# Row-order dt kept in SBUF, permutes in other slots, and the residual summed in PSUM, in a two-layer Metaformer kernel

## The chip, the cores and the metric

The kernel runs on one core of a Trainium2 chip. Five engines work side by side, each through its own queue of instructions in order: TensorE (PE, matmuls), VectorE (DVE), ScalarE (ACT), GpSimd (POOL) and SyncE (SP), which here issues nearly all DMAs. They wait for each other by semaphores. The metric is the device time of a whole execution in microseconds (us), the median over several runs.

## The reference

The input is one image of 64×64 positions with 96 channels. Layer 0 and layer 1 each add a mixer with state-space scans and then an MLP. The change lies in layer 1, whose mixer is, cut to what matters:

```python
xz = x @ W_in.T                                   # 96 -> 2 x 192
xp, z = xz[..., :192], xz[..., 192:]
xc = silu(conv3x3(xp) + conv_b)                   # dense, 192 -> 192 channels
xs = [row order, column order, and both reversed] # 4 sequences of L = 4096
dts, Bs, Cs = split(x_proj_w @ xs, [6, 16, 16])
delta = softplus(dt_proj_w @ dts + dt_proj_b)     # "dt", one per channel and position
A = -exp(A_logs)                                  # 192 x 16 states
# for each sequence, step by step:
h = exp(delta * A) * h + delta * u * B            # 16 states per channel
y = sum(h * C over states) + D * u
# the four sequences' y are put back in row order and added
out = (yy * silu(z)) @ W_out.T                    # 192 -> 96, "out_proj"
x = x + out                                       # the residual
```

The MLP after it normalizes x, rounds to eight-bit and sixteen-bit floats and adds its result to x.

## The kernel before, in words

**Stages.** Layer 0 comes first. Layer 1 then computes the convolution and, in `project_chunks`, the projections, softplus, dt and du (= u·dt), in two halves of 32 image rows: chunks of 512 positions (`CH`), four to a half. `project_chunks` goes through `for i in range(3)`: i = 0 and 1 are channels 0 to 127 in the first and second 1024 positions of the half, i = 2 is channels 128 to 191 of all 2048, folded on the partitions. It writes dt (row order, and `dtc` in column order), du, B and C to DRAM. The scan stage `scans` reads them again, and the `tail` does out_proj of the last channels and the MLP.

**Scan stage.** The 192 channels are cut in 6 groups of 32 (`NG`, `GC`), the 16 states in quarters: a tile has 32 channels × 4 states on its 128 partitions, and a group takes 4 passes, 24 passes in all (numbered 0 to 23). One pass has 16 slots, and one slot is one DVE scan of 128×1024 values (`tensor_tensor_scan`, L1261):

| slots | what is scanned | written to |
|---|---|---|
| 0–3 | columns, one way | h1s |
| 4–7 | columns, the other way | xws, in place |
| 8–11 | rows, one way | h0s |
| 12–15 | rows, the other way | x0s, x1s or x2s, in place |

`xs[i % 3]` holds B·du of pass i in row order (x0s, x1s, x2s in the trace); xws is its copy in column order, made by `permute` (L1240) in four parts. Each scan needs a decay factor `da` = exp(A·dt), made by ACT from dt1s (column order) or dt0s (row order) in PSUM with two buffers (`decay`, L1250); slots 4 and 12 use the one of the slot before.

**Around the scans.** In each pass, POOL adds the two column scans to hss, back in row order (`add_columns`, L1266, four parts, from h1s and xws). PE adds hss, h0s and x through an identity matrix into PSUM (`add_all`, L1274, tile `hs`, two buffers), ACT copies that out (`fetch`, L1280), POOL multiplies by C (`times_c`), and PE sums the states (`sum_states`). POOL also multiplies B by du for coming passes (`times_b`, L1234).

**Order.** The order on each engine is written out by hand: `keep` holds an instruction in program order on its engine. A table `plan` says in which slot, counted from a pass's own slot 0, each step is issued; a negative slot lies in the pass before, one of 16 or more in the pass after. In each slot the scan is issued first, then `decay` of the next slot, then what the plan lists:

```python
spots(permute, -7, -6, -5, -4)        # ACT, for the next pass: its slots 9 to 12
spots(add_columns, 5, 6, 7, 8)        # POOL
spots(add_all, 13, 15, 18, 20)        # PE, fetches of ACT between slots 15 and 24
```

**Pass 0.** Before the first scan, dt1s of group 0 is spread from `dtc` within SBUF to the four partitions of each channel (`spread`, L1058 to L1060), and dus from du likewise. dt0s of group 0 is loaded from DRAM, by `load_dt(0, 0)` (L1439), four DMAs of 512 KB issued by SP after all stores. SP's DMAs are taken in order: those of `project_chunks`, then these.

**Early out_proj.** In passes 17 to 23, y of the finished groups is read back (`load_y`, tile ye), multiplied by its weights (`early_out`, L1381, tile eo), copied by ACT (`early_fetch`, L1386, tile et) and added by POOL to the residual `res` (`early_add`, L1389). f = 0 stands for channels 0 to 127 from pass 17 on, two chunks to a pass, f = 1 for the next 32 from pass 21 on, three to a pass. Channels 160 to 191 follow in the tail.

Of the kernel before, what the change touches and what calls it, by code (L numbers as in the profile page):

```python
# [108 lines left out]
class Net:  # L109
# [24 lines left out]
    def column(self, name, value):  # L134
        t = self.cp.tile([P, 1], F32, tag=name, name=name)
        self.nc.gpsimd.memset(t, value)
        return t
# [550 lines left out]
    def softplus(self, sp, z, dt, n, name, last=None):  # L688

        nc = self.nc  # L690
        nc.scalar.activation(z, z, AF.Sigmoid, bias=self.nln2, scale=-1.0)
        zz = sp.tile([P, n], F32, tag="zz", name=f"zz{name}")
        nc.scalar.activation(zz, z, AF.Square)
        p = sp.tile([P, n], F32, tag="p", name=f"p{name}")
        nc.vector.tensor_scalar(p, zz, LOG1P[4], None, ALU.mult)
        for i in (3, 2, 1):
            nc.vector.scalar_tensor_tensor(p, p, LOG1P[i], zz, ALU.add, ALU.mult)
        nc.vector.scalar_tensor_tensor(p, p, LOG1P[0], z, ALU.add, ALU.mult)
        (last or nc.vector).tensor_tensor(dt, dt, p, ALU.add)

        return p
# [220 lines left out]
    def layer1(self, w, pool):  # L922
        nc, tc = self.nc, self.tc
        self.bc_d = [self.scratch("bc1", [2, NST, L])]
        self.dt_d = [self.scratch(f"dt1{o}", [DI, L]) for o in range(2)]
        self.du_d, self.y_d = self.scratch("du1", [DI, L]), self.scratch("y1", [DI, L])
        self.u_d = [self.scratch(f"u1{g}", [GP[g], L]) for g in range(2)]

        gp = pool.enter_context(tc.tile_pool(name="first", bufs=1))
        self.du, self.dt1 = (gp.tile([P, L], F32, tag=t, name=f"{t}s") for t in ("du", "dt1"))  # L930
        with ExitStack() as ctx:
            dp = ctx.enter_context(tc.tile_pool(name="dtc1", bufs=1))
            sp = ctx.enter_context(tc.tile_pool(name="sp1", bufs=2))
            kp = ctx.enter_context(tc.tile_pool(name="sg1", bufs=3))
            up = [ctx.enter_context(tc.tile_pool(name=f"u1{i}", bufs=1)) for i in range(2)]
# [5 lines left out]
            self.project_chunks(sp, ps, self.conv_chunks(kp, ps, pc, up, 0), 0)  # L941
# [5 lines left out]
            self.project_chunks(sp, ps, u, 4, xs)  # L947
        return xs
# [83 lines left out]
    def project_chunks(self, sp, ps, u, c, xs=None):  # L1032
# [37 lines left out]


        for i in range(3):
# [40 lines left out]
            if xs and i < 2:  # L1113

                for m in range(2):
                    t = ps.tile([P, CH], F32, tag="cw", name=f"du4{i}{m}")
                    nc.tensor.matmul(t, self.spread4, du[0:GC, chunk(m)], start=True, stop=True)
                    x = xs[0][:, chunk(c + first + m)]
                    keep(nc.vector.tensor_tensor(x, x, t, ALU.mult))
            for h in range(1 + g):  # L1120
                r = LANES[h] if g else slice(0, P)
                to = slice(g * P, g * P + r.stop - r.start)
                k = c + first + 2 * h
                at = slice(k * CH, k * CH + n)
                if g == 0:
                    spread(self.du[:, at], du)
                if xs and i == 1:
                    for j in range(1, NS):
                        spread(self.dt1[:, j * SC : (j + 1) * SC], self.dtc[0][:, j * SC : (j + 1) * SC])
                    self.load_b(1, xs[1], half[1])  # L1130
                else:
                    by_column(g, dt[r], k, 1)
                keep(dma(self.dt_d[0][to, at], dt[r]))
                rows = slice(0, GP[1]) if g else slice(GC, P)
                keep(dma(self.du_d[g * P + rows.start : g * P + rows.stop, at], du[r if g else rows]))
        if xs:
            keep(dma(self.dt_d[1][GC:P], self.dtc[0][GC:P]))
            keep(dma(self.dt_d[1][P:DI], self.dtc[1]))
# [21 lines left out]
    def scans(self, xs, out):  # L1160
# [14 lines left out]
        with ExitStack() as ctx:  # L1175
# [7 lines left out]
            st = [inner.enter_context(tc.tile_pool(name=t, bufs=1)) for t in ("dt0", "h1", "xw")]  # L1183
# [8 lines left out]
            dt0, h1, xw = (p.tile([P, L], F32, tag=t, name=f"{t}s") for p, t in zip(st, ("dt0", "h1", "xw")))  # L1192
            du, dt1 = self.du, self.dt1
# [172 lines left out]
            early, inputs, partial, taken = {}, {}, {}, {}  # L1366

            def load_y(f, m):
                rows = (slice(0, P), slice(P, P + GC))[f]
                if f == 0 or m == 0:  # L1370
                    self.ye = gp.tile([P, CH], F32, tag="ye", name=f"ye{f}{m}")
                to = slice(GC * (m % 3), GC * (m % 3) + GC) if f else slice(0, P)
                inputs[f, m] = self.ye[to], self.tail_w[f][to]
                keep(nc.sync.dma_start(self.ye[to], self.y_d[rows, chunk(m)]))

            def early_out(f, m):
                y, w = inputs.pop((f, m))
                t = ph.tile([P, CH], F32, tag="hs", name=f"eo{f}{m}")
                o = t[:, 0 : 4 * CD].rearrange("p (j d) -> p j d", j=4)
                for j in range(4):  # L1380
                    keep(nc.tensor.matmul(o[:, j], y[:, j:CH:4], w, start=True, stop=True))  # L1381
                partial[f, m] = o

            def early_fetch(f, m):
                taken[f, m] = gp.tile([P, 4, CD], F32, tag="et", name=f"et{f}{m}")
                keep(nc.scalar.copy(taken[f, m], partial.pop((f, m))))  # L1386

            def early_add(f, m):
                keep(nc.gpsimd.tensor_tensor(self.res[:, m], self.res[:, m], taken.pop((f, m)), ALU.add))  # L1389
# [36 lines left out]
            spots(permute, -7, -6, -5, -4)  # L1426
# [12 lines left out]
            load_dt(0, 0)  # L1439
# [364 lines left out]
```

## Time and profile before

| | |
|---|---|
| median of 3 runs | 1580.23 us (1579.53 to 1580.86) |
| profiled execution | 1580.6 us |
| its span in the profile | 1578.7 us, 1.9 us lie around it |
| mean granted TensorE clock | 0.81 |
| DVE busy | 1188.7 us (75%) |
| PE busy | 1194.0 us (76%) |
| ACT busy | 890.5 us (56%) |
| POOL busy | 825.9 us (52%) |
| column scans into h1s, 72 of 96 | 169.2 us, 2350 ns each |
| hss adds on POOL | 96 of 2373 ns |

The profile is one execution. Its rows give the start and the time in us, the engine, the line, the tiles written and read (`out<-in`), their shape and, in square brackets, how long the engine was idle before the row and what it was released by. "x4" means four such instructions in one row. SPq rows are DMA issues. The busy shares are means over all stages, so what a change in one stage is worth is read in that stage.

### The profile page before, as it was taken

The numbers are of one execution on the slowest core, as the hardware profiler recorded it, in microseconds if no ns is written. First come the engines' busy times: TensorE is split into PE (matmuls) and PEld (weight loads), VectorE is DVE, ScalarE is ACT, GpSimd is POOL, SyncE is SP. The second block draws the span as 40 slices with busy tenths as digits, with TensorE's granted clock in tenths as the row PEclk, the third lists the DMA queues.
The fourth block names the chain that finished last, engine by engine and source line by source line (L and its number), as shares of the span: only waits on it lengthen the run. The fifth ranks groups of instructions, "written<-read, shape, count | busy, mean of one in ns | idle before, by whom it ended". The sixth has DMA issues, their size and how long they took to land.

```text
span 1578.7 us, 12397 instructions
## 1 busy us (share of the span) xinstructions
PE 1194.0 (76%) x3728; PEld 487.3 (31%) x3728; DVE 1188.7 (75%) x895; ACT 890.5 (56%) x1058; POOL 825.9 (52%) x482
## 2 busy tenths in 40 slices
PE   5969788779999317777777777777777776778875
PEld 2512254434342002222222222222222332333343
DVE  5487344430321859999999999999999998989965
ACT  4233333330422637777777777677777776777535
POOL 1001122110011457776877787777877876886545
PEclk9988666679999558888888888888888887978865
DMA  2032200000132583545555455635564556352201
GB/s 68 1 97 75 56 1 10 21 13 27 23 112 86 150 263 121 183 161 173 150 170 192 141 150 170 202 131 150 170 223 124 158 183 232 120 155 82 83 1 40
DMA packets 65616, 184.20 MB, mean 117 GB/s; under 512 B 21072, under 2 KB 35044, under 8 KB 58596
## 3 DMA queue, kind: packets, MB, share of 16 engines
q1 hardware_dynamic: 63352, 183.03, 37.5%
q8 instruction: 31, 0.51, 0.1%
q10 hardware_dynamic: 2188, 0.29, 0.1%
q14 instruction: 45, 0.37, 0.1%
HBM read 158.07 MB, written 20.99 MB: 113 GB/s over the span
## 4 chain that ended last, share of the span: by engine, by line
DVE 38%; PE 25%; issue 7%; ACT 7%; POOL 5%; DMA 3%; SPq 3%; DVEq 1%; POOLq 0%; ACTq 0%
DVE h1s L1261 10%; DVE xws L1261 10%; DVE h0s L1261 8%; PE hs L1274 5%; PE cv L996 4%; DVE x0s L1261 3%; DVE x2s L1261 3%; DVE x1s L1261 2%; ACT da L1250 2%; ACT xws L1240 2%; PE cv L1001 2%; PE o L455 1%; PE o L454 1%; SPq L1211 1%; PE in L285 1%
## 5 line engine op out<-in xcount | busy, mean ns | idle before, releaser
L1266 POOL TENSOR_TENSOR hss<-h1s,xws 128x1024 f32<-128x1024 f32 x96 | 224.4, 2373 | 139.9 <-PE hs L1274 137.2
L1250 ACT ACTIVATE da<-dt1s,a 128x1024 f32<-128x1024 f32 x168 | 187.8, 1118 | 143.6 <-DVE xws L1261 81.6
L1274 PE MATMUL hs<-hss,ident 128*128 128x512 f32 x376 | 213.1, 650 | 55.8 <-DMA dt0s<-dt 36.0
L1250 ACT ACTIVATE da<-dt0s,a 128x1024 f32<-128x1024 f32 x168 | 187.1, 1115 | 81.2 <-DVE xws L1261 49.6
L1261 DVE TENSOR_TENSOR_SCAN xws<-da,xws 128x1024 f32<-128x1024 f32 x96 | 224.2, 2335 | 8.3
L1274 PE MATMUL hs<-h0s,ident 128*128 128x512 f32 x376 | 198.7, 611 | 14.7 <-DVE h0s L1261 14.7
L1261 DVE TENSOR_TENSOR_SCAN h1s<-da,h1s,xws 128x1024 f32<-128x1024 f32 x72 | 169.2, 2350 | 12.7 <-ACT da L1250 4.5
L1274 PEld LDWEIGHTS hs<-hss,ident 128*128 128x128 f32 x376 | 68.7, 200 | 188.6 <-issue 80.1
L1274 PEld LDWEIGHTS hs<-h0s,ident 128*128 128x128 f32 x376 | 75.0, 200 | 112.9 <-issue 93.8
L1295 PE MATMUL acc<-hc2s,fold 128*32 128x512 f32 x128 | 47.2, 826 | 56.1 <-POOL hc2s L1284 53.0
L1295 PE MATMUL acc<-hc0s,fold 128*32 128x512 f32 x128 | 47.6, 834 | 51.4 <-POOL hc0s L1284 51.4
L1234 POOL TENSOR_TENSOR x2s<-x2s,dus 128x1024 f32<-128x1024 f32 x32 | 75.2, 2360 | 10.9 <-DMA x2s<-bc 10.9
L1295 PE MATMUL acc<-hc1s,fold 128*32 128x512 f32 x128 | 46.1, 810 | 45.8 <-POOL hc1s L1284 45.8
L1261 DVE TENSOR_TENSOR_SCAN x1s<-da,x1s 128x1024 f32<-128x1024 f32 x32 | 74.7, 2335 | 7.5 <-ACT da L1250 5.2
L1261 DVE TENSOR_TENSOR_SCAN x0s<-da,x0s 128x1024 f32<-128x1024 f32 x32 | 74.7, 2335 | 7.2 <-ACT da L1250 4.9
L1112 POOL TENSOR_TENSOR p<-u,dt 128x1024 f32<-128x1024 f32 x6 | 15.1, 2523 | 122.5 <-ACT z L1099 102.7
L1261 DVE TENSOR_TENSOR_SCAN x2s<-da,x2s 128x1024 f32<-128x1024 f32 x32 | 74.7, 2335 | 4.2 <-ACT da L1250 1.7
L1234 POOL TENSOR_TENSOR x1s<-x1s,dus 128x1024 f32<-128x1024 f32 x32 | 75.1, 2359 | 2.6 <-DMA x1s<-bc 2.5
L1274 PE MATMUL hs<-x0s,ident 128*128 128x512 f32 x128 | 67.1, 606 | 0.2 <-DVE x0s L1261 0.2
L1381 PE MATMUL eo<-two,ye 128*128 128x96 f32 (+1 forms) x128 | 30.9, 424 | 48.0 <-DMA ye<-y 37.8
L390 POOL TENSOR_TENSOR ua<-acc,sga 128x512 f32<-128x512 f32 x4 | 5.8, 1453 | 117.2 <-DMA u<-uc 115.5
L1234 POOL TENSOR_TENSOR x0s<-x0s,dus 128x1024 f32<-128x1024 f32 x28 | 65.8, 2363 | 0.0
(310 smaller groups left out, 2628.3 us busy)
## 6 DMA issues: line engine op xcount, KB each, us to landing
c0s<-bc SPq DMA_DIRECT2D x184, 128.0 KB
c1s<-bc SPq DMA_DIRECT2D x184, 128.0 KB
x2s<-bc SPq DMA_DIRECT2D x32, 512.0 KB
x0s<-bc SPq DMA_DIRECT2D x28, 512.0 KB
x1s<-bc SPq DMA_DIRECT2D x28, 512.0 KB
dus<-du SPq DMA_DIRECT2D x20, 512.0 KB
dt1s<-dt SPq DMA_DIRECT2D x40, 256.0 KB
dt0s<-dt SPq DMA_DIRECT2D x40, 256.0 KB
```

Of the source, the lines that this page charges most:

```text
L285: keep(nc.tensor.matmul(t, self.w_in[:, g * P : (g + 1) * P], xt, start=True, stop=True))
L454: keep(nc.tensor.matmul(t[:, j, :], y[0][:, at[0]], w[0], start=True, stop=False))
L996: nc.tensor.matmul(t, cw[0][:, tap, 0:P], image(0, slice(0, P), n, tap), start=tap == 0, stop=False)
L1001: nc.tensor.matmul(t, cw[1][r, tap, 0:P], image(1, r, n, tap), start=False, stop=tap == 8)
L1234: keep(nc.gpsimd.tensor_tensor(x, x, du[:, part[j]], ALU.mult))
L1240: keep(copy(grid(xw)[:, w, :], cols(xs[i % 3])[:, w, :]))
L1250: keep(nc.scalar.activation(das[i, s], dts[o][:, part[j]], AF.Exp, scale=self.a6[:, g, k : k + 1]))
L1261: keep(nc.vector.tensor_tensor_scan(to, da, x, start, ALU.mult, ALU.add))
L1266: keep(nc.gpsimd.tensor_tensor(cols(hs)[:, w, :], grid(h1)[:, w, :], grid(xw)[:, w, :], ALU.add))
L1274: keep(nc.tensor.matmul(t, self.ident, x[:, chunk(m)], start=x is hs, stop=x is xs[i % 3]))
L1295: keep(nc.tensor.matmul(to, self.fold4, src, start=k == 0, stop=k == NK - 1))
L1381: keep(nc.tensor.matmul(o[:, j], y[:, j:CH:4], w, start=True, stop=True))
```

## The change

Five things are changed.

- In `project_chunks`, dt of the first group in row order is spread within SBUF to dt0s, four DMAs for each 1024 positions, as dus is; the load from DRAM before the scans goes, and dt0s moves to the pool "first". Only channels 32 to 127 of dt are stored for the row order. Softplus's instructions are kept in program order (on DVE always, on ACT for i = 0), the last add of dt is done by DVE for i = 2 as well, x_proj of the second two chunks is issued after the first softplus, products of x0s come one round later, and a6 is negated by ACT. The stores of dt and du of i = 1 in the second half come last. du has its own tile.
- In the plan, `permute` is issued three slots earlier for its first part and one slot earlier for the others: in slots 6, 9, 10 and 11 of the pass before.
- In the early out_proj, PE adds the residual by an identity matmul into the same PSUM tile, and ACT copies the sum to `res`; `early_add` and et are gone. ye has two buffers and is loaded in earlier slots.
- The tail's pool has three buffers instead of four.
- The constant columns share a tile.

```diff
@@ -685,20 +687,23 @@
                     nc.sync.dma_start(self.du_d[g][:, at], du)
-    def softplus(self, sp, z, dt, n, name, last=None):
-        nc = self.nc
-        nc.scalar.activation(z, z, AF.Sigmoid, bias=self.nln2, scale=-1.0)
+    def softplus(self, sp, z, dt, n, name, p=None, keep=(None, None)):
+        nc = self.nc
+        act, dve = (k or (lambda instruction: None) for k in keep)
+        act(nc.scalar.activation(z, z, AF.Sigmoid, bias=self.nln2, scale=-1.0))
         zz = sp.tile([P, n], F32, tag="zz", name=f"zz{name}")
-        nc.scalar.activation(zz, z, AF.Square)
-        p = sp.tile([P, n], F32, tag="p", name=f"p{name}")
-        nc.vector.tensor_scalar(p, zz, LOG1P[4], None, ALU.mult)
+        act(nc.scalar.activation(zz, z, AF.Square))
+        if p is None:
+            p = sp.tile([P, n], F32, tag="p", name=f"p{name}")
+        dve(nc.vector.tensor_scalar(p, zz, LOG1P[4], None, ALU.mult))
         for i in (3, 2, 1):
-            nc.vector.scalar_tensor_tensor(p, p, LOG1P[i], zz, ALU.add, ALU.mult)
-        nc.vector.scalar_tensor_tensor(p, p, LOG1P[0], z, ALU.add, ALU.mult)
-        (last or nc.vector).tensor_tensor(dt, dt, p, ALU.add)
-        return p
+            dve(nc.vector.scalar_tensor_tensor(p, p, LOG1P[i], zz, ALU.add, ALU.mult))
+        dve(nc.vector.scalar_tensor_tensor(p, p, LOG1P[0], z, ALU.add, ALU.mult))
+        dve(nc.vector.tensor_tensor(dt, dt, p, ALU.add))
     def scan_group(self, g):
@@ layer1
-        self.du, self.dt1 = (gp.tile([P, L], F32, tag=t, name=f"{t}s") for t in ("du", "dt1"))
+        self.du, self.dt0, self.dt1 = (gp.tile([P, L], F32, tag=t, name=f"{t}s") for t in ("du", "dt0", "dt1"))
...
+            so = ctx.enter_context(tc.tile_pool(name="so1", bufs=2))
@@ -1029,7 +1037,7 @@
         return u
-    def project_chunks(self, sp, ps, u, c, xs=None):
+    def project_chunks(self, so, sp, ps, u, c, xs=None):
@@ -1043,13 +1051,21 @@
                 self.load_b(k, xs[k], half[0])
-        def x_proj(k):
-            h, s = place(k)
-            r = LANES[h]
-            t = ps.tile([P, CH], F32, tag="ps", name=f"xd1{c}{k}")
-            nc.tensor.matmul(t[0:XW], self.w_x[0], u[0][:, chunk(k)], start=True, stop=False)
-            nc.tensor.matmul(t[0:XW], self.w_x[1][r], u[1][r, chunk(s)], start=False, stop=True)
-            nc.scalar.copy(self.xd[:, chunk(k)], t[0:XW])
+        def x_proj(first):
+            for k in (first, first + 1):
+                h, s = place(k)
+                r = LANES[h]
+                t = ps.tile([P, CH], F32, tag="ps", name=f"xd1{c}{k}")
+                nc.tensor.matmul(t[0:XW], self.w_x[0], u[0][:, chunk(k)], start=True, stop=False)
+                nc.tensor.matmul(t[0:XW], self.w_x[1][r], u[1][r, chunk(s)], start=False, stop=True)
+                keep(nc.scalar.copy(self.xd[:, chunk(k)], t[0:XW]))
+            at = slice(first * CH, first * CH + n)
+            here = slice((c + first) * CH, (c + first) * CH + n)
+            for k in range(2):
+                keep(dma(self.bc_d[0][k, :, here], self.xd[(XB, XC)[k] : (XB, XC)[k] + NST, at]))
+            if xs:
+                self.load_b(0, xs[0], here)
         def times_b(j):
...
@@ -1068,22 +1084,20 @@
                 keep(copy(to[:, w], dt[:, w]))
+        late, ready = [], []
+        def product(x, t):
+            return lambda: keep(nc.vector.tensor_tensor(x, x, t, ALU.mult))
         for i in range(3):
...
             bias = self.vec[g][:, 1:2]
-            if i < 2:
-                at = slice(first * CH, first * CH + n)
-                here = slice((c + first) * CH, (c + first) * CH + n)
-                x_proj(first)
-                x_proj(first + 1)
-                for k in range(2):
-                    keep(dma(self.bc_d[0][k, :, here], self.xd[(XB, XC)[k] : (XB, XC)[k] + NST, at]))
-                if xs:
-                    self.load_b(0, xs[0], here)
+            if i == 0:
+                x_proj(0)
             z = sp.tile([P, n], F32, tag="z", name=f"z1{c}{i}")
-            dt = sp.tile([P, n], F32, tag="dt", name=f"dt1{c}{i}")
+            dt = so.tile([P, n], F32, tag="dt", name=f"dt1{c}{i}")
             for m in range(2):
...
@@ -1098,14 +1112,20 @@
                 nc.scalar.activation(dt[:, s], t, AF.Relu, bias=bias)
-            du = self.softplus(sp, z, dt, n, f"1{c}{i}", nc.gpsimd if i == 2 else nc.vector)
+            du = so.tile([P, n], F32, tag="du", bufs=3, name=f"du1{c}{i}")
+            self.softplus(sp, z, dt, n, f"1{c}{i}", du, (keep if i == 0 else None, keep))
+            for f in ready:
+                f()
+            ready = []
+            if i == 0:
+                x_proj(2)
             if xs and i == 0:
...
                 times_b(1)
-            elif xs and i == 2:
+            if xs and i == 2:
                 keep(nc.scalar.activation(self.a6, self.a6, AF.Exp))
-                keep(nc.gpsimd.tensor_scalar(self.a6, self.a6, -1.0, None, ALU.mult))
+                keep(nc.scalar.activation(self.a6, self.a6, AF.Copy, scale=-1.0))
             if xs and i == 1:
...
@@ -1115,25 +1135,32 @@
                     nc.tensor.matmul(t, self.spread4, du[0:GC, chunk(m)], start=True, stop=True)
-                    x = xs[0][:, chunk(c + first + m)]
-                    keep(nc.vector.tensor_tensor(x, x, t, ALU.mult))
+                    ready.append(product(xs[0][:, chunk(c + first + m)], t))
             for h in range(1 + g):
                 r = LANES[h] if g else slice(0, P)
-                to = slice(g * P, g * P + r.stop - r.start)
                 k = c + first + 2 * h
                 at = slice(k * CH, k * CH + n)
-                if g == 0:
-                    spread(self.du[:, at], du)
                 if xs and i == 1:
...
                         spread(self.dt1[:, j * SC : (j + 1) * SC], self.dtc[0][:, j * SC : (j + 1) * SC])
+                    spread(self.du[:, at], du)
                     self.load_b(1, xs[1], half[1])
+                    spread(self.dt0[:, at], dt)
                 else:
+                    if g == 0:
+                        spread(self.du[:, at], du)
+                        spread(self.dt0[:, at], dt)
                     by_column(g, dt[r], k, 1)
-                keep(dma(self.dt_d[0][to, at], dt[r]))
                 rows = slice(0, GP[1]) if g else slice(GC, P)
-                keep(dma(self.du_d[g * P + rows.start : g * P + rows.stop, at], du[r if g else rows]))
+                for d, t in ((self.dt_d[0], dt), (self.du_d, du)):
+                    store = (d[g * P + rows.start : g * P + rows.stop, at], t[r if g else rows])
+                    if xs and i == 1:
+                        late.append(store)
+                    else:
+                        keep(dma(*store))
         if xs:
+            for store in late:
+                keep(dma(*store))
             keep(dma(self.dt_d[1][GC:P], self.dtc[0][GC:P]))
...
@@ -1363,12 +1390,12 @@
                         keep(nc.sync.dma_start(to[q], gu[GC * q : GC * q + GC]))
-            early, inputs, partial, taken = {}, {}, {}, {}
+            early, inputs, partial = {}, {}, {}
             def load_y(f, m):
...
                 if f == 0 or m == 0:
-                    self.ye = gp.tile([P, CH], F32, tag="ye", name=f"ye{f}{m}")
+                    self.ye = gp.tile([P, CH], F32, tag="ye", bufs=2, name=f"ye{f}{m}")
                 to = slice(GC * (m % 3), GC * (m % 3) + GC) if f else slice(0, P)
...
@@ -1377,24 +1404,22 @@
                 o = t[:, 0 : 4 * CD].rearrange("p (j d) -> p j d", j=4)
+                keep(nc.tensor.matmul(o, self.ident, self.res[:, m], start=True, stop=False))
                 for j in range(4):
-                    keep(nc.tensor.matmul(o[:, j], y[:, j:CH:4], w, start=True, stop=True))
+                    keep(nc.tensor.matmul(o[:, j], y[:, j:CH:4], w, start=False, stop=j == 3))
                 partial[f, m] = o
             def early_fetch(f, m):
-                taken[f, m] = gp.tile([P, 4, CD], F32, tag="et", name=f"et{f}{m}")
-                keep(nc.scalar.copy(taken[f, m], partial.pop((f, m))))
-            def early_add(f, m):
-                keep(nc.gpsimd.tensor_tensor(self.res[:, m], self.res[:, m], taken.pop((f, m)), ALU.add))
+                keep(nc.scalar.copy(self.res[:, m], partial.pop((f, m))))
             for f, i0, spots in (
-                (0, n - 7, ((4, 8, 10, 12), (8, 11, 13, 14))),
-                (1, n - 3, ((4, 8, 10, 12), (5, 9, 12, 13), (8, 11, 13, 14))),
+                (0, n - 7, ((0, 8, 10), (2, 11, 13))),
+                (1, n - 3, ((1, 8, 9), (2, 9, 11), (4, 11, 13))),
             ):
...
                     i, s = divmod(m, len(spots))
-                    for do, at_slot in zip((load_y, early_out, early_fetch, early_add), spots[s]):
+                    for do, at_slot in zip((load_y, early_out, early_fetch), spots[s]):
                         early.setdefault((i0 + i, at_slot), []).append((do, (f, m)))
...
@@ -1423,7 +1448,7 @@
             spots(times_b, -20, -19, -16, -14)
-            spots(permute, -7, -6, -5, -4)
+            spots(permute, -10, -7, -6, -5)
             spots(add_columns, 5, 6, 7, 8)
...
@@ -1436,7 +1461,6 @@
             spots(load_c, 10, 12, 18, 21)
-            load_dt(0, 0)
             for j in range(2):
...
@@ -1504,7 +1528,7 @@
-        tp = ctx.enter_context(tc.tile_pool(name="at1", bufs=4))
+        tp = ctx.enter_context(tc.tile_pool(name="at1", bufs=3))
```

More of the change, by code (lines that the diff above doesn't have):

```diff
@@ L134, in column @@
     def column(self, name, value):
-        t = self.cp.tile([P, 1], F32, tag=name, name=name)
+        if not hasattr(self, "columns"):
+            self.columns = iter(self.cp.tile([P, 8], F32, tag="columns", name="columns").rearrange("p (n o) -> n p o", o=1))
+        t = next(self.columns)
         self.nc.gpsimd.memset(t, value)
@@ L929, in layer1 @@
         gp = pool.enter_context(tc.tile_pool(name="first", bufs=1))
-        self.du, self.dt1 = (gp.tile([P, L], F32, tag=t, name=f"{t}s") for t in ("du", "dt1"))
+        self.du, self.dt0, self.dt1 = (gp.tile([P, L], F32, tag=t, name=f"{t}s") for t in ("du", "dt0", "dt1"))
         with ExitStack() as ctx:
             dp = ctx.enter_context(tc.tile_pool(name="dtc1", bufs=1))
+            up = [ctx.enter_context(tc.tile_pool(name="u10", bufs=1))]
+            so = ctx.enter_context(tc.tile_pool(name="so1", bufs=2))
             sp = ctx.enter_context(tc.tile_pool(name="sp1", bufs=2))
             kp = ctx.enter_context(tc.tile_pool(name="sg1", bufs=3))
-            up = [ctx.enter_context(tc.tile_pool(name=f"u1{i}", bufs=1)) for i in range(2)]
+            up.append(ctx.enter_context(tc.tile_pool(name="u11", bufs=1)))
             ps = ctx.enter_context(tc.tile_pool(name="ps_b1", bufs=2, space=PSUM))
@@ L940, in layer1 @@
             self.weights1(up[1], w)
-            self.project_chunks(sp, ps, self.conv_chunks(kp, ps, pc, up, 0), 0)
+            self.project_chunks(so, sp, ps, self.conv_chunks(kp, ps, pc, up, 0), 0)
             u = self.conv_chunks(kp, ps, pc, up, 4)
@@ L946, in layer1 @@
             xs = [xp.tile([P, L], F32, tag=f"x{m}", name=f"x{m}s") for m in range(3)]
-            self.project_chunks(sp, ps, u, 4, xs)
+            self.project_chunks(so, sp, ps, u, 4, xs)
         return xs
@@ L1181, in scans @@
             inner = ctx.enter_context(ExitStack())
-            st = [inner.enter_context(tc.tile_pool(name=t, bufs=1)) for t in ("dt0", "h1", "xw")]
+            st = [inner.enter_context(tc.tile_pool(name=t, bufs=1)) for t in ("h1", "xw")]
             pa = inner.enter_context(tc.tile_pool(name="ps_da", bufs=2, space=PSUM))
@@ L1191, in scans @@
             hs, h0 = (hh.tile([P, L], F32, tag=t, name=f"{t}s") for t in ("hs", "h0"))
-            dt0, h1, xw = (p.tile([P, L], F32, tag=t, name=f"{t}s") for p, t in zip(st, ("dt0", "h1", "xw")))
-            du, dt1 = self.du, self.dt1
+            h1, xw = (p.tile([P, L], F32, tag=t, name=f"{t}s") for p, t in zip(st, ("h1", "xw")))
+            du, dt0, dt1 = self.du, self.dt0, self.dt1
             dts = [dt0, dt1]
```

## The prediction

> **What bounds the kernel now.** I read the page first, then the timelines of one early pass, of the middle of pass 0 and of the late passes, then the waits. On the page:
>
> ```profile
> PE 1194.0 (76%) x3728; PEld 487.3 (31%) x3728; DVE 1188.7 (75%) x895; ACT 890.5 (56%) x1058; POOL 825.9 (52%) x482
> DVE 38%; PE 25%; issue 7%; ACT 7%; POOL 5%; DMA 3%; SPq 3%; DVEq 1%; POOLq 0%; ACTq 0%
> ```
>
> VectorE (DVE) leads the chain, and about 927 of the 1579 us are its 384 scans: they start 2.41 us apart, 38.6 us to a pass of 16. DVE is then busy nearly without a gap, so the scan stage changes only through a gap that opens or closes on DVE. Its largest gap is in pass 0:
>
> ```profile
> 561.29 8.75 SPq L1211 DMA_DIRECT2D dt0s<-dt  x4
> 562.98 9.29 POOL L1266 TENSOR_TENSOR hss<-h1s,xws 128x1024 f32<-128x1024 f32 x4 [2.77 <-DMA du<-p]
> ...
> 578.18 2.15 ACT L1250 ACTIVATE da<-dt0s,a 128x1024 f32<-128x1024 f32 x2 [17.56 <-DMA dt0s<-dt]
> 579.38 2.29 DVE L1261 TENSOR_TENSOR_SCAN h0s<-da,x0s 128x1024 f32<-128x1024 f32 x1 [15.01 <-DMA x2s<-bc]
> ```
>
> The scan of slot 8 stands idle 15.01 us. The row names x2s, but `da` beside it waited for the load of dt0s (issued at 561.29, landed by 578.18). A steady pass, here pass 2, has no such gap:
>
> ```profile
> 652.45 9.36 POOL L1266 TENSOR_TENSOR hss<-h1s,xws 128x1024 f32<-128x1024 f32 x4 [6.06 <-PE hs L1274]
> ...
> 654.46 1.12 ACT L1250 ACTIVATE da<-dt0s,a 128x1024 f32<-128x1024 f32 x1 [1.33 <-DVE xws L1261]
> ...
> 656.80 2.26 DVE L1261 TENSOR_TENSOR_SCAN h0s<-da,x2s 128x1024 f32<-128x1024 f32 x1
> ...
> 660.59 1.93 ACT L1240 COPY xws<-x0s 128x1024 f32<-128x1024 f32 x1
> ```
>
> ScalarE (ACT) makes slot 8's `da` at 654.46 and starts the permutes at 660.59, in slot 9. POOL's four hss adds run from 652.45 to 661.81; they read xws, which the permutes overwrite. In the late passes out_proj opens gaps:
>
> ```profile
> 1331.16 2.15 PE L1381 MATMUL eo<-two,ye 128*128 128x96 f32 x8 [15.06 <-DMA ye<-y]
> ...
> 1333.40 0.48 ACT L1386 COPY et<-eo 128x384 f32<-128x384 f32 x1 [4.84 <-PE eo L1381]
> ...
> 1334.94 2.35 DVE L1261 TENSOR_TENSOR_SCAN x1s<-da,x1s 128x1024 f32<-128x1024 f32 x1 [3.78 <-ACT da L1250]
> ...
> 1412.06 0.48 ACT L1386 COPY et<-eo 128x384 f32<-128x384 f32 x1 [1.45 <-POOL res L1389]
> ...
> 1413.59 2.35 DVE L1261 TENSOR_TENSOR_SCAN x0s<-da,x0s 128x1024 f32<-128x1024 f32 x1 [2.30 <-ACT da L1250]
> ```
>
> A late ye, or an `et` not yet added, holds ACT; ACT holds `da`; `da` holds the scan.
>
> **What the skill says.** The Trainium skill, "SBUF — State Buffer", section "Who interferes with whom": a DVE operation with two SBUF inputs and a GpSimd operation that reads SBUF exclude each other for a whole instruction. The trace agrees: the first softplus STT, issued at 511.40 beside a POOL multiply that ends at 513.56, is in a group of three taking 5.76 us where later ones take 3.74. "PSUM — Partial Sum Buffer", section "PSUM: the matmul accumulator": a matmul marked as first overwrites, later ones add; no row of before adds a residual that way. "TensorE: Matmul & The Clock Gate", section "Part 1: The HAM clock gate": half clock when idle, full after sustained work; here a 512-column fp32 pair takes 1.02 us at full clock and 2.07 us cold (1415.85).
>
> **Part A, dt0 within SBUF.** It removes the 512 KB load (four issues, 8.75 us of SP) and adds 8 SBUF-to-SBUF DMAs of 32 rows, queued before dt2, du2 and the late stores.
>
> - First scan, at 543.29: it waits for `da`, which waits for a6 behind a POOL add (538.73) and the negation (1.06 us at 541.04). With the negation on ACT, idle for 8.74 us there, DVE's own chain decides. It ends with the first permute at 541.96; x_proj of the second half comes earlier, so its idle 1.62 at 532.77 goes, and the dt add comes to it, 1.22: 541.56. The products of x0s move one round later and the softplus keeps its order, the same instructions: nothing, hidden in DVE's own queue. I take 541.6: 1.7 us gained (0 to 3).
> - Slots 1 to 3 of pass 0 lose .83, .68 and .56, sum 2.07, to the first permutes, which alternate with `da` on ACT (1.94 and 1.12). Those four permutes stay, but slot 0 starts earlier than they do now, so I keep 2.07 as recovered only in the bound: slot 8 could start between 562.7 (579.38 − 15.01 − 1.7) and 560.6.
> - It is held anyway. Pass 1's first permute now stands before slot 8's `da` on ACT and waits for hss, and hss waits for the last store of du to land (issue 557.36, hss 562.98: 5.6 us). SP's queue after, from the page's issue times: the first dt1s loads no longer stand behind bc and x0s, so they go at 530.7 instead of 535.19; 16 of them take 10.4 us (541.1), four dus 2.5, four x1s 2.6, four dt0s 2.5 (548.7), dt2 and du2 twice 2.8 (551.5), late dt1 .5, so the late du store goes at 552 and lands at 557.6. hss part 0 is 557.6 to 560.0; plus 3.03 (next part): slot 8 at ≈563.0.
>
> Gain 579.38 − 563.0 = **16.4 us**, between 13 and 18.5 (560.9). Its cover: dt0s of the second row half, issued by 548.7, has 12 us to land; past 561 the gap returns one for one (rival 3).
>
> **Part C, permutes at slots 6, 9, 10, 11.** In the changed program's order of instructions, ACT has slot 7's `da`, permute, slot 8's `da`, fetch. The permute waits for hss part 0 of the same pass. Behind it on ACT stand `da` of slot 8, two fetches and z's copies; DVE's slot 8 waits for that `da`. In pass 2: hss part 0 ends 652.45 + 2.37 = 654.82; + .04 + 1.84 (permutes start 1.84 before the `da` behind them) + 1.12 + .03 = 657.85, where slot 8 began at 656.80. Stall **1.05 us**. Could hss go earlier? It is released by PE's last read of hs, on the chain slot 4's scan end → `da` → fetch (ends +1.67) → hs<-hss (+2.25 its last start) → hss +2.93; adding 2.37 + .04 + 1.84 + 1.15 gives +8.33 against slot 8's +7.28: again 1.05. It recurs, since everything after slot 8 shifts with it.
>
> Where PE runs cold, hss is later. From each pass's row, hss part 0's end less slot 8's start, plus 3.03: passes 1 to 18 give 1.11, 1.06, 1.05, 1.06, 1.78, 2.19, 1.05, 1.05, 1.78, 1.06, 1.06, 1.06, 3.48, 3.82, 1.79, 1.54, 1.78, 2.18: **29.9 us lost** (floor 18 × 1.05 = 18.9). Passes 19 to 22 give 2.64, 4.14, 2.70, 3.13 = 12.6, partly from out_proj waits that Part B removes: I take **10** (4.2 to 13). Nothing in return is on the path: pass 1's permutes were long done by its first scan.
>
> **Part B, residual in PSUM.** Gone: 16 POOL adds (about 1.0 us each) and ACT's wait for them; ye is loaded 3 to 6 slots earlier (7 to 14 us), into two buffers. DVE's gaps in passes 17 to 23, read off the timeline, sum to 13.9 us (3.78, 2.30 and 2.00 the largest). I take **12** as gained (8 to 13.9). Added: 16 identity matmuls of 384 columns, two fp32 passes each, .65 us (384/512 of two of .43) = 10.4 us on PE. No row of before shows one; they stand in slots 8 and 11, where PE has no scan sum to make, so I cost them at nothing; without that cover up to 10.4 (double when cold) would reach hss. A gain is excluded: they replace no PE work.
>
> Tail buffers 4 to 3 and the shared constant columns: nothing, since their groups' order on each engine stays.
>
> **Sum.** −16.4 + 29.9 + 10 − 12 = +11.5 on a profiled execution of 1580.6 us (span 1578.7 and 1.9 around it): 1592.1. The median is 0.4 lower, so **1591.7**.
>
> **Rivals.**
>
> 1. *Faster: PE stays warm.* Every stall is at the floor: 22 × 1.05 = 23.1, pass 0 −18.5, late gaps −13.9: −9.3, about 1571. The sign turns where the mean stall of the 22 passes is (16.4 + 12) / 22 = 1.29 us; I have 1.81. For it: 9 of the 22 stand at the floor. Against: the clock averages 0.81 in before, and nothing added in the early passes keeps PE busier. Chance .11.
> 2. *PE becomes the bound*: residual matmuls on a cold PE push hss back in passes 17 to 22, +10 more, about 1602. For it: the waits of eo come with a cold PE (the 2.07 pair). Against: they stand where PE waits for scans. Chance .20.
> 3. *The spread is late*: dt0s or the late stores land 8 us later than worked out, so pass 0 gains 8, about 1600. For it: the windows view has the 16 DMA engines busy 0.96 of 545 to 580, and the dt0s load took 17 us. Against: that load's traffic is what goes. Chance .15.
> 4. *It doesn't do what it says*: with a permute that waits for nothing, −28.4 stays, about 1552. For it: ACT idles 1.33 us ahead of slot 8's `da` in pass 2. Against: the order on ACT and the xws that hss and permute share. Chance .04.
>
> **How the numbers follow.** My case has .44 and a result within my small terms of no change .06. A measurement of this kernel tells about 0.2%, 3.2 us. Faster: rivals 1 and 4, .15. Same: the .06 and the .04 of my case whose stalls lie between floor and table, .10. Slower: .40 + .20 + .15 = .75. The range, 1575 to 1606, runs from halfway between rival 1 and no change to a little past rival 2; some .15 lies outside.
>
> **What would show it.** Right: the first h0s scan of most passes idles 1 us or more, released by ACT `da`; ACT's first permute idles about 1.7 us, released by POOL hss; pass 0's gap is about 2 us; no POOL res rows, no wait of eo for ye. Wrong: that permute starts without idling, slot 8 has no gap from pass 2 on, or pass 0 keeps over 8 us.

## The result, and the profile after

The changed kernel takes 1601.15 us (median of 4 runs, 1597.56 to 1604.15) against 1579.88 us before (4 runs, 1573.18 to 1580.86): a ratio of 1.0143, 95% interval 1.0106 to 1.0180. It is 21 us slower by the medians, and lies within the range given. Its profiled execution, the slowest of the four, took 1604.15 us, span 1602.3, which is 23.6 us above the span before. The page's line of busy times:

```profile
PE 1240.0 (77%) x3760; PEld 504.1 (31%) x3760; DVE 1199.0 (75%) x897; ACT 891.9 (56%) x1059; POOL 805.6 (50%) x463
```

DVE sets the pace of the scans. The scans themselves take the same time in both kernels (the page has 169.2 us for those into h1s and 224.2 us for those into xws, before and after), so what the scan stage loses is idle time of DVE. The waits (who waited for whom: us in total, times, longest) name it:

```profile
ACT xws L1267 <- POOL hss L1293: 68.7, 23, 5.2
DVE h0s L1288 <- ACT da L1277: 48.3, 24, 4.4
```

Neither wait is among those before. ACT's permute waits for POOL's hss in the 23 passes 0 to 22, and in all of them the first row scan then stands idle behind the `da` queued after that permute. (The view puts one of these idle times, in pass 5, down to a DMA, and counts two short ones of slot 11.) The timeline of pass 2 after, whose rows before stand in the prediction:

```profile
637.79 9.35 POOL L1293 TENSOR_TENSOR hss<-h1s,xws 128x1024 f32<-128x1024 f32 x4 [6.06 <-PE hs L1301]
...
640.20 1.96 ACT L1267 COPY xws<-x0s 128x1024 f32<-128x1024 f32 x1 [1.73 <-POOL hss L1293]
642.06 1.11 ACT L1277 ACTIVATE da<-dt0s,a 128x1024 f32<-128x1024 f32 x1
...
643.21 2.29 DVE L1288 TENSOR_TENSOR_SCAN h0s<-da,x2s 128x1024 f32<-128x1024 f32 x1 [0.98 <-ACT da L1277]
```

The permute starts 2.41 us after hss part 0 did (its 2.37 and .04), `da` 1.86 later and the scan 1.15 after that. So the scan comes 5.42 us after hss began, where it came 4.35 us after it before (652.45 to 656.80): 1.07 us are lost at slot 8. The same in the middle of pass 0:

```profile
551.75 0.78 SPq L1163 DMA_DIRECT2D du<-du  x1
...
558.37 9.33 POOL L1293 TENSOR_TENSOR hss<-h1s,xws 128x1024 f32<-128x1024 f32 x4 [4.81 <-DMA du<-du]
560.77 1.93 ACT L1267 COPY xws<-x1s 128x1024 f32<-128x1024 f32 x1 [4.80 <-POOL hss L1293]
562.60 2.15 ACT L1277 ACTIVATE da<-dt0s,a 128x1024 f32<-128x1024 f32 x2
563.81 2.29 DVE L1288 TENSOR_TENSOR_SCAN h0s<-da,x0s 128x1024 f32<-128x1024 f32 x1 [4.09 <-ACT da L1277]
```

The gap of 15.01 us has become one of 4.09, now released by `da` and not by a load. In the late passes, POOL's adds and PE's wait for ye are gone from the views, and the residual is there as a matmul (instructions of one line and shape together: busy us, mean ns of one, idle time before them):

```profile
L1408 PE MATMUL eo<-res,ident 128*128 128x384 f32 x32 | 22.9, 814 | 9.3 <-ACT hc0s L1307 4.2 <-ACT hc1s L1307 3.8 <-ACT hc2s L1307 1.3
L1410 PE MATMUL eo<-two,ye 128*128 128x96 f32 (+1 forms) x128 | 32.7, 423 | 0.0
```

The difference of the two spans, taken apart at the start of scans, in us:

| stretch | before | after | difference |
|---|---|---|---|
| to slot 8 of pass 0 | 579.4 | 563.8 | −15.6 |
| slot 8 of pass 0 to slot 0 of pass 1 | 19.3 | 19.3 | 0.0 |
| passes 1 to 18 | 696.3 | 735.5 | +39.2 |
| passes 19 to 22 | 164.8 | 167.5 | +2.7 |
| pass 23 and the tail | 119.0 | 116.3 | −2.7 |

### The profile page after: what moved, and what is told of

It is laid out like the page before. It is cut to its first block, busy times and chain, and to the rows that moved or that the text cites. A ratio compares the mean times of both kernels' runs of the same rounds, so it can differ in the third digit from the quotient of the medians.

```text
span 1602.3 us, 12430 instructions
## 1 busy us (share of the span) xinstructions
PE 1240.0 (77%) x3760; PEld 504.1 (31%) x3760; DVE 1199.0 (75%) x897; ACT 891.9 (56%) x1059; POOL 805.6 (50%) x463
## 5 line engine op out<-in xcount | busy, mean ns | idle before, releaser
L1301 PE MATMUL hs<-hss,ident 128*128 128x512 f32 x376 | 220.2, 669 | 78.9 <-POOL hss L1293 34.0
L1288 DVE TENSOR_TENSOR_SCAN xws<-da,xws 128x1024 f32<-128x1024 f32 x96 | 224.2, 2335 | 8.3
L1301 PE MATMUL hs<-h0s,ident 128*128 128x512 f32 x376 | 207.2, 635 | 3.7 <-DVE h0s L1288 3.7
L1288 DVE TENSOR_TENSOR_SCAN h1s<-da,h1s,xws 128x1024 f32<-128x1024 f32 x72 | 169.2, 2350 | 10.4 <-ACT da L1277 1.3
L1132 POOL TENSOR_TENSOR du<-u,dt 128x1024 f32<-128x1024 f32 x6 | 15.0, 2503 | 134.9 <-DVE dt L706 134.9
L1267 ACT COPY xws<-x1s 128x1024 f32<-128x1024 f32 x32 | 62.2, 1966 | 25.6 <-POOL hss L1293 25.6
L1267 ACT COPY xws<-x2s 128x1024 f32<-128x1024 f32 x32 | 62.4, 1971 | 23.9 <-POOL hss L1293 23.9
L1322 PE MATMUL acc<-hc1s,fold 128*32 128x512 f32 x128 | 44.7, 786 | 39.8 <-POOL hc1s L1311 39.8
L1322 PE MATMUL acc<-hc0s,fold 128*32 128x512 f32 x128 | 43.6, 767 | 40.8 <-POOL hc0s L1311 40.7
L1267 ACT COPY xws<-x0s 128x1024 f32<-128x1024 f32 x31 | 60.7, 1974 | 22.7 <-POOL hss L1293 19.2
L1301 PE MATMUL hs<-x0s,ident 128*128 128x512 f32 x128 | 71.0, 638 | 0.3 <-DVE x0s L1288 0.2
```

What stands on the lines that cost most here:

```text
L1132: keep(nc.gpsimd.tensor_tensor(du, u[g][:, first * CH : first * CH + n], dt, ALU.mult))
L1267: keep(copy(grid(xw)[:, w, :], cols(xs[i % 3])[:, w, :]))
L1288: keep(nc.vector.tensor_tensor_scan(to, da, x, start, ALU.mult, ALU.add))
L1301: keep(nc.tensor.matmul(t, self.ident, x[:, chunk(m)], start=x is hs, stop=x is xs[i % 3]))
L1322: keep(nc.tensor.matmul(to, self.fold4, src, start=k == 0, stop=k == NK - 1))
```

## The experiments

**Theory.** The order on ACT costs the time: a permute that waits for hss stands ahead of the `da` of slot 8. The rest of the change gains. **Rival.** The added work on PE, or a later hss, costs the time wherever the permutes stand.

**e1: the permutes back in their slots.**

```diff
-            spots(permute, -10, -7, -6, -5)
+            spots(permute, -7, -6, -5, -4)
```

> The changed kernel with the permutes back in slots 9 to 12. Theory (the first permute, put ahead of slot 8's da on ACT, costs the stalls read in passes 1 to 22 of the changed kernel, 49 us in all, and holds slot 8 of pass 0 by some 3 us): 1601 - 49 - 3 = about 1549, between 1546 and 1556; the first h0s scan of passes 1 to 22 idles less than 0.1 us, and slot 8 of pass 0 idles 1 to 2 us. Rival (the loss is PE's, from the residual matmuls and a later hss, whatever the permutes do): 1590 to 1601, with the stalls still there.

Measured: 1546.45 us (7 runs), ratio to before 0.9793, interval 0.9767 to 0.9820. The timeline of its pass 2 has `da` 2.34 us ahead of the scan, no idle time at the scan, and the permute in slot 9:

```profile
620.77 1.12 ACT L1277 ACTIVATE da<-dt0s,a 128x1024 f32<-128x1024 f32 x1 [1.34 <-DVE xws L1288]
...
623.11 2.26 DVE L1288 TENSOR_TENSOR_SCAN h0s<-da,x2s 128x1024 f32<-128x1024 f32 x1
...
626.90 1.96 ACT L1267 COPY xws<-x0s 128x1024 f32<-128x1024 f32 x1
```

All 22 stalls (the idle time of slot 8 in passes 1 to 22) are gone, and with them the rival's second half. So one line of the plan costs some 55 us, and the rest of the change is worth 33: of the three kernels, this is the fastest. Slot 8 of pass 0 had no gap at all (19.26 us after slot 0, as in any pass), where I had expected 1 to 2 us. Its profiled execution, at 1537.91, is the fastest of the seven. Slot 0 of pass 0 started at 526.7 in it and at 540.4 in that of the changed kernel, though the code up to there is the same; in the profiles of e3, e4 and e9, which share that code too, it started at 540.4, 527.7 and 535.3. So the stages are compared from slot 0 on: 1009.4 us against 1062.0. That is 52.6 us less, about what the stalls (49.0 us) and the 4.2 us that pass 0 lost add up to.

**e2: the permutes' slots alone, in the kernel before.**

```diff
-            spots(permute, -7, -6, -5, -4)
+            spots(permute, -10, -7, -6, -5)
```

> The kernel before with nothing but the permutes in slots 6, 9, 10 and 11. Theory: pass 0 loses nothing, as the dt0 load holds slot 8 there for longer; passes 1 to 22 lose 40 to 50 us, so 1620 to 1630, with the late gaps of the out_proj still there beside them. Rival (the loss is of the residual matmuls): 1580 to 1590, since those are not in it.

Measured: 1619.17 us (6 runs), ratio 1.0247, interval 1.0216 to 1.0279. With no residual matmul in it, the same two waits appear:

```profile
ACT xws L1240 <- POOL hss L1266: 57.9, 21, 5.1
DVE h0s L1261 <- ACT da L1250: 42.0, 21, 4.3
```

The rival's first half falls with this. Stalls of slot 8 sum to 44.9 us over passes 1 to 22, within the 40 to 50 expected, and the median is 40 above before, just under the range given.

**e3: the first permute one slot later.**

```diff
-            spots(permute, -10, -7, -6, -5)
+            spots(permute, -9, -7, -6, -5)
```

> The changed kernel with only the first permute one slot later: in slot 7, so behind slot 8's da on ACT and ahead of slot 9's. Theory (what costs is the order of permute and da, not an early permute as such): in the steady passes hss part 0 ends 1.98 us before slot 8 starts, so the permute ends 0.1 before it and slot 9's da 1.0 after it, 1.4 us before slot 9 needs it: no stall there, and only in passes where hss is later by more than 1.4 us a part of it remains: 1550 to 1562. Rival (any permute that waits for hss costs what its wait costs, wherever it stands): 1590 to 1601.

Measured: 1553.58 us (6 runs), ratio 0.9841, interval 0.9806 to 0.9875. Its pass 2:

```profile
636.73 1.12 ACT L1277 ACTIVATE da<-dt0s,a 128x1024 f32<-128x1024 f32 x1 [1.34 <-DVE xws L1288]
...
638.26 2.09 ACT L1267 COPY xws<-x0s 128x1024 f32<-128x1024 f32 x1
639.06 2.26 DVE L1288 TENSOR_TENSOR_SCAN h0s<-da,x2s 128x1024 f32<-128x1024 f32 x1
640.24 1.13 ACT L1277 ACTIVATE da<-dt0s,a 128x1024 f32<-128x1024 f32 x1
```

Letting one `da` pass on ACT gives back most of the loss: slot 8 does not stall in any pass. It stays 7 us above e1 by the medians, and 11.6 us from slot 0 on in the profiles (1021.0 to 1009.4), since slot 9 and the slots behind it wait where the permute ends late (waits of h0s for `da` of 18.8 us in all in the profile). It is the place in ACT's queue that costs.

**e4: a warm PE.** In the changed kernel, stalls exceed the least one of 1.06 us in 12 of 22 passes. A pair of 512-column matmuls takes 1.02 us in most rows and 1.9 to 2.1 us in some; I call the second "cold". The theory was that PE begins its `add_all` cold.

```diff
+            def warm(i, s):
+                o, way, back, j = slot(i, s - 1)
+                t = ph.tile([P, CH], F32, tag="hs", name=f"warm{i}_{s}")
+                for h in range(2):
+                    m = j * (SC // CH) + h
+                    keep(nc.tensor.matmul(t, self.ident, h0[:, chunk(m)], start=True, stop=True))
...
+                    if s in (9, 10, 11):
+                        warm(i, s)
```

> The changed kernel with two more 512-column identity matmuls on PE in each of slots 9, 10 and 11 (138 in all, read from h0s after its scan, into an hs buffer that nothing reads), where PE otherwise stands idle. Theory (in the changed kernel stalls above the floor of 1.05 us come from a PE that starts its add_all of slot 13 at a low clock): hss comes earlier relative to slot 8, stalls fall from 49 to some 28, since passes 5, 9, 13, 17 and 21 keep a part for ACT's copy of acc in slot 14: 1575 to 1590. Rival (the excess is PE's amount of work, or the wait of ACT for POOL): no gain or a loss, 1600 to 1615.

Measured: 1608.31 us (7 runs), ratio 1.0190, interval 1.0162 to 1.0219. The mean granted clock rose from .81 to .85 (profiled executions), and the stalls of passes 1 to 18 stayed: 39.8 us against 38.7. The theory falls as I put it: a cold PE ahead of slot 13 is not what makes hss late. (That this kernel is even slower comes from elsewhere: its passes 21 and 22 take 8.4 us longer, since the added matmuls stand ahead of out_proj's on PE and slot 15 waits 6.4 and 6.9 us for `da`, where it waited .7 and .8.) The changed kernel's PE rows show the place. Of the chains of six chunks ahead of hss, that of pass 3 (second row below) begins without idling and that of pass 4 (sixth row) after 2.87 us of it; the first and fifth rows are the first chunk of `add_all` in the pass before each:

```profile
654.36 2.08 PE L1301 MATMUL hs<-hss,ident 128*128 128x512 f32 x2
...
661.90 1.12 PE L1301 MATMUL hs<-hss,ident 128*128 128x512 f32 x2
662.86 1.02 PE L1301 MATMUL hs<-h0s,ident 128*128 128x512 f32 x2
663.72 1.02 PE L1301 MATMUL hs<-x2s,ident 128*128 128x512 f32 x2
...
693.04 1.12 PE L1301 MATMUL hs<-hss,ident 128*128 128x512 f32 x2
...
701.63 1.13 PE L1301 MATMUL hs<-hss,ident 128*128 128x512 f32 x2 [2.87 <-ACT hc0s L1307]
702.60 1.66 PE L1301 MATMUL hs<-h0s,ident 128*128 128x512 f32 x2
704.05 1.91 PE L1301 MATMUL hs<-x0s,ident 128*128 128x512 f32 x2
705.75 1.28 PE L1301 MATMUL hs<-hss,ident 128*128 128x512 f32 x2
```

In pass 2, `add_all`'s first chunk ran cold, and the first two lasted until the fetch; in pass 3 both ran at the usual speed, ended early, and PE stood idle until the fetch of slot 15. Its next pairs take 1.66 and 1.91 us where 1.02 is usual, and the last hs<-hss starts 16.29 us after the chain's begin, not 14.94: 1.35 us more, and the stall goes from 1.07 to 2.39. In e4, `add_all` begins at the usual speed in pass 2 as well: the chain ahead of pass 3's hss now has a pause of 2.00 us, its next pairs are slow, and that stall too is 2.38.

**e9: an earlier first fetch.** It tests that reading: the first fetch of most passes is issued one slot earlier.

```diff
-            for m, s in enumerate((15, 16, 17, 19, 20, 21, 23, 24)):
+            def fetch_first(i, early):
+                if early != (i > 0 and ends_group(i - 1)):
+                    fetch(i, 0, 0)
+            plan.setdefault(14, []).append((fetch_first, (True,)))
+            plan.setdefault(15, []).append((fetch_first, (False,)))
+            for m, s in enumerate((16, 17, 19, 20, 21, 23, 24), 1):
```

> The changed kernel with its permute slots, but the first fetch of a pass in slot 14 instead of 15, except in the five passes after a group's end (there the buffer is taken). Theory: what makes stalls longer than 1.05 us is that PE, after the first two chunks of add_all, stands idle about 3 us until that fetch and then runs its next chunk at low clock, 1.33 us longer; with the fetch earlier PE does not idle, so the stalls of passes 4, 7, 10, 14, 18, 19 and 22 (18 us in the changed kernel) fall to about 1.06 each, and those of 5, 9, 13, 17 and 21 stay: some 10 us less, 1588 to 1594. Rival (PE's clock drops wherever it drops, or ACT waits for the chunk in slot 14 and delays da): stalls the same or more, 1600 to 1606.

Measured: 1596.74 us (6 runs), ratio 1.0102, interval 1.0071 to 1.0133, which overlaps that of the changed kernel. The stalls of passes 7, 10 and 14 fell from 2.4 to 1.06, and those of 8, 12 and 16 rose from 1.07 to 2.27, so that passes 1 to 18 sum to 38.5 against 38.7. The pause had moved one chunk on, to the fetch of slot 16, and pairs slowed behind it, here ahead of pass 8's hss:

```profile
861.74 1.12 PE L1301 MATMUL hs<-hss,ident 128*128 128x512 f32 x2 [1.97 <-ACT hc1s L1307]
862.70 1.84 PE L1301 MATMUL hs<-h0s,ident 128*128 128x512 f32 x2
```

So it is inconclusive as a remedy. The slow pairs follow a pause within the chain in both kernels, but not every pause has them: after one of 2.17 us ahead of pass 20's hss in the changed kernel, and one of 2.85 us ahead of pass 5's in the kernel before, all pairs take the usual 1.02. Which passes they fall on is not settled.

**e5: dt0 within SBUF, without the other two parts.** The changed kernel with the permutes and the whole early out_proj (ye, et, POOL's adds, the load slots) as before. The tail's three buffers and the shared columns stay in it.

```diff
-            spots(permute, -10, -7, -6, -5)
+            spots(permute, -7, -6, -5, -4)
...
-                keep(nc.tensor.matmul(o, self.ident, self.res[:, m], start=True, stop=False))
...
+                keep(nc.gpsimd.tensor_tensor(self.res[:, m], self.res[:, m], taken.pop((f, m)), ALU.add))
```

> The changed kernel without its permute slots and without its out_proj part: what is left is dt0 within SBUF and the work around it (with the tail's buffers and the shared columns). Theory: pass 0 has no gap at slot 8, so it is 16.8 us shorter than in the kernel before, and the first scan starts 2 to 3 us earlier: 19 to 20 us faster than before, 1558 to 1562; the late gaps of passes 17 to 23 are those of before. Rival (the gain of pass 0 returns as a later hss or dt1 load): 1566 to 1575.

Measured: 1557.43 us (6 runs), ratio 0.9859, interval 0.9831 to 0.9887: 22 us faster by the ratio. Pass 0 takes 38.49 us from slot 0 to slot 0, and 55.35 before: 16.9 us; the rest lies ahead of the first scan (543.3 to 536.7), where single executions of one code differ by more than that. Pass 23 and the tail take 118.8 us, and 119.0 before, so the tail's buffers cost nothing that shows. The waits of the late passes are those of before:

```profile
PE eo L1409 <- DMA ye<-y: 38.3, 5, 15.3
ACT et L1414 <- POOL res L1417: 10.1, 4, 5.3
```

**e7 and e10: the residual in PSUM, ye as before.** e7 is e1 with one ye buffer and the old load slots.

```diff
-                    self.ye = gp.tile([P, CH], F32, tag="ye", bufs=2, name=f"ye{f}{m}")
+                    self.ye = gp.tile([P, CH], F32, tag="ye", name=f"ye{f}{m}")
...
-                (0, n - 7, ((0, 8, 10), (2, 11, 13))),
-                (1, n - 3, ((1, 8, 9), (2, 9, 11), (4, 11, 13))),
+                (0, n - 7, ((4, 8, 10), (8, 11, 13))),
+                (1, n - 3, ((4, 8, 9), (5, 9, 11), (8, 11, 13))),
```

> The same with the residual summed in PSUM, but with one ye buffer, loaded in the slots of before (4 and 8; 4, 5 and 8). Theory: the waits of ACT for POOL's adds go, those of PE for ye stay (3.8 us in pass 19 and parts of passes 20 to 22), so about half of the 13 us that the out_proj part brings: 1549 to 1555, between e5 and e1 (1546). Rival (the 16 residual matmuls cost what the saved adds bring): no faster than e5, 1558 to 1562.

Measured: 1560.90 us (6 runs), ratio 0.9880, interval 0.9850 to 0.9910: not the 1549 to 1555 expected, but the rival's time. Yet its passes 17 to 23 and the tail take 356.7 us, between e5's 362.0 and e1's 352.3. The loss is in pass 0, where hss and the scan of slot 8 start within .1 us of each other, after a long wait:

```profile
564.11 2.29 DVE L1288 TENSOR_TENSOR_SCAN h0s<-da,x0s 128x1024 f32<-128x1024 f32 x1 [8.62 <-DMA x2s<-bc]
564.21 9.34 POOL L1293 TENSOR_TENSOR hss<-h1s,xws 128x1024 f32<-128x1024 f32 x4 [14.97 <-DMA x2s<-bc]
```

Without et (4 × 96 floats a partition) the tiles behind it lie 1536 bytes lower than in e5. e10 keeps an unused tile of et's size:

```diff
+            gp.tile([P, 4, CD], F32, tag="et", name="et")
```

> The kernel of e7 (dt0 within SBUF, residual in PSUM, ye in one buffer at the old slots) with an unused tile of et's size kept in its pool, so that hs, h0 and the tiles behind them lie at the addresses of e5. In e7 the slot 8 scan of pass 0 stands idle 8.6 us beside hss, and its hs starts at byte 112512 of a partition, within dtc (up to 113248), whose store is in flight. Theory: that overlap made e7 slow; without it pass 0 is 38.5 us and the rest is e7's: 8 to 9 us less than e7's 1561, 1550 to 1554. Rival (PSUM residual costs what it brings): no change, 1558 to 1562.

Measured: 1552.59 us (6 runs), ratio 0.9833, interval 0.9800 to 0.9866. The wait is gone from the same rows:

```profile
556.35 9.34 POOL L1293 TENSOR_TENSOR hss<-h1s,xws 128x1024 f32<-128x1024 f32 x4 [3.90 <-DVE xws L1288]
...
558.61 2.26 DVE L1288 TENSOR_TENSOR_SCAN h0s<-da,x0s 128x1024 f32<-128x1024 f32 x1
```

Nothing but the unused tile differs, so where the tiles lie is what cost e7 its time: 8.3 us by the medians, 8.7 by pass 0 in the profiles (47.23 to 38.49 us). The traces also show which transfer was waited for. In e7, DVE and POOL each stand, ahead of the rows shown, at a wait that ends at 563.77 and names the same semaphore; its last update, at 563.74, is the landing of the last store of dtc (L1165, issued at 550.62). In e10 that store landed at 566.30, long after slot 8 had begun.

From the start of pass 17 to the end e5 takes 362.0 us, e10 356.5 and e1 352.3. So the out_proj part divides into some 5.5 us for the residual in PSUM and 4.2 us for ye's loads and buffer, read from one profile each; the medians give 5 and 6, with intervals that overlap.

## Why the prediction was right, and where its size was off

- **The sign and its mechanism held.** The permute's wait for hss, the `da` behind it and the scan of slot 8 came as worked out: 1.07 us in pass 2 and pass 3, for 1.05, and the permute's own wait was 1.73 us, for about 1.7. e2 shows that this alone makes the kernel before slower, e1 that without it the change is faster, and e3 that the order on ACT is what counts.
- **The size did not hold.** My own case gave +11.5 us; measured are 21 by the medians and 23.6 by the spans. That 1601 lies within 1575 to 1606 is owed to the width kept for other cases. It stands beside the 1602 of rival 2 and the 1600 of rival 3, but came about by neither's path (below).
- **Pass 0**: 15.6 us gained for 16.4. The late du store was issued at 551.75, for 552 worked out; hss part 0 ended at 560.73, for 560.0, and slot 8 began at 563.81, for 563.0. The first scan came at 540.37, for 541.6; that this is so close is partly luck, since with the same code it came anywhere from 526.7 to 540.4. The gap of slot 8 was 4.09 us and not about 2: slots 1 to 3 lost nothing, so slot 8 could have started at 559.6. That the permute's wait takes back what the load had given is shown by e1, in which slot 8 does not wait.
- **Passes 1 to 18: the term that was mis-sized.** I had 29.9 us from the table of hss in the kernel before; the stalls are 38.7. The least stall was right, in 9 of 18 passes. The table assumed that each pass keeps the lateness it had. It did not: pass 4 went from 1.06 to 2.39 and pass 7 from 1.05 to 2.38, while pass 6 fell from 2.19 to 1.06 and pass 14 from 3.82 to 2.40. Of the 8.8 us of excess, 6.9 lie in passes 5, 9, 13 and 17, each the second of its group (1.78 to 3.45, 1.78 to 3.46, 3.48 to 4.39, 1.78 to 4.39). The first fetch ahead of their hss is held 1.01 us by POOL in both kernels, but the pause of PE grew from 1.7 to 2.9 us before to 2.0 to 4.0 us, and slow pairs follow it in all four, where before they followed it in pass 13 alone. That the longer period, 39.7 us for 38.6, moves the slow pairs is my reading and not shown. Why the new pattern has more of them is open; e4 and e9 changed where they fall, not their sum.
- **Passes 19 to 22**: stalls of 10.3 us, for 10.
- **Late gaps**: from the start of pass 19 to the end both kernels take 283.8 us, so with stalls of 10.3 in it 10.3 is gained, for 12. e1, without stalls, takes 274.1 us there: 9.7 gained. The residual matmuls cost PE 22.9 us of busy time and not 10.4, since they ran at 814 ns each; 10.4 doubled, as the prediction had it for a cold PE, is near that. Their own cost on the path is not isolated; that summing in PSUM gains more than they cost is borne out by e10 against e5 (356.5 to 362.0 us from pass 17 on).
- The sum was +11.5; with the measured terms it is −15.6 + 39.2 + 10.3 − 10.3 = +23.6, the difference of the spans (39.2 is what passes 1 to 18 grew, 38.7 of it stalls). Rival 1, a stall at its floor everywhere, failed on 12 of the 22 passes. Rival 2 put the excess on residual matmuls; 7.2 of the 8.8 us came in passes 1 to 17, whose hss lies ahead of the first of them. Rival 3 had pass 0 gain 8 us, and it gained 15.6. Rival 4 had a permute that waits for nothing, and it waited in 23 passes.

The Trainium skill, "TensorE: Matmul & The Clock Gate", section "HAM oscillation — how this bites in real kernels", warns of idle gaps above about 3.4 us that throw PE back to half clock in every round. The traces agree that slow pairs come after gaps, but not with the length: pairs slowed after gaps of 2.87 us (changed kernel) and 1.97 us (e9), and did not after one of 2.85 us (kernel before, ahead of pass 5's hss). The measurement decides: here the length of a gap alone does not tell.

## What to carry to other kernels

When an instruction is moved earlier in an engine's fixed order, look at what it waits for and at what stands behind it: here a copy needed only in the next pass, moved ahead of an activation needed at once, cost more than all other parts of the change gained. A table of lateness taken from one kernel need not hold in the next: here it was 8.8 us short of 38.7. Take the least and the worst pass as the range.

## What the runs showed that I had not expected

- A change of 1536 bytes in where tiles lie cost 8.3 us (e7 against e10), because a tile came to wait for the store of another that had lain at its address.
- PE kept busier, with the mean granted clock at .85 for .81, was no faster where it mattered: its pairs slowed after the pause inside the chain.
- The time up to the first scan differs by 14 us (526.7 to 540.4) between five executions of the same code, so a gain ahead of it can't be read from one profile of each kernel.
